# Holding both scatter-adds of an expert to one place in the GpSimd queue of a one-core attention and mixture-of-experts kernel

## The chip, the core and the metric

The kernel runs on one core of one Trainium2 chip. The metric is the device time of one launch in microseconds (us), taken as the median of repeated runs. The profile shown here is one separate profiled execution of the same kernel.

## What is computed

The input `x` is 4 x 2048 x 512 float32, so 8192 tokens of 512 numbers. The output is `x` plus two branches, both of which read the layer-normalised tokens `xn`:

- an attention-like branch with 512 random features: `feats = exp(xn . proj - |xn|^2 correction)`, the same for a 512 x 512 weight matrix, and the product of the two;
- a mixture of 64 experts plus one shared expert. The router gives 64 scores per token; the best 4 of 8 groups of experts are kept, then the best 8 experts. An expert has 256 slots (`CAP`), which are given to its tokens in the order of the tokens; later ones are dropped.

In short form:

```python
g = einsum('ech,ehi->eci', dispatch, gate_w)
u = einsum('ech,ehi->eci', dispatch, up_w)
expert_out = einsum('eci,eih->ech', silu(g) * u, down_w)
output = zeros((t, h)).at[tidx].add(expert_out[flat_e, pos_c] * weight)
output += (silu(tokens @ shared_gate_w) * (tokens @ shared_up_w)) @ shared_down_w
x = x + attention(xn) + output
```

`dispatch` holds the tokens' rows sorted to expert and slot. The line with `.at[tidx].add` is the one that the change is about: each expert's 256 result rows are added to the rows of the output that belong to its tokens.

## The kernel before, in words

**Numbers.** All products are float32. An operand is split into an upper part in float32r (`upper`, L98, a ScalarE copy) and the rest (`rest`, L101, a VectorE subtraction), and `products` (L104) does three TensorE matmuls for each product. So TensorE lines in a profile mostly stand at L109, and the two split helpers at L99 and L102; the tiles' names tell what they belong to.

**Stages.** First the tokens are normalised, routed and counted in 16 blocks of 512 (`look_up`, `dense`); for half of the blocks the shared expert and the attention are finished there, for seven of the others the attention is left for later (`late_attention`), and what they need is kept in DRAM. Then comes the expert stage, a loop over `i` from 0 to 64 (L881), with pieces of the left-over attention between the experts. At the end the rest of the blocks is finished (`ends`): it reads the output rows back, adds the shared expert and the attention, and writes them.

**The expert loop.** Iteration `i` traces, in this order: the loads of weights ahead of time; the hidden layer of expert `i` (`hidden`, TensorE, tile `ps_gu`); one step of `slots` (`seek`), which issues two lookups on GpSimd (`find`, L656, tile `at`) for expert `i + 9`; the gather of the token rows of expert `i + 4` (`gather`, L709, tile `xg`, two indirect DMAs of 128 rows, one of four buffers); the transposes of expert `i + 1` (`turn_slots`, L724, tile `ps_t`); a share of the left-over attention; and `down(i - 1)`: for each half of 128 slots the second layer (tile `ps_e`), its scaling by ScalarE into `ye` (L773, three buffers of both halves), and the sum, an indirect DMA that adds the 128 rows to the output in DRAM (L774).

Every fourth step of `seek` also traces `tokens_of` (L664): five VectorE operations that turn the looked-up counts of four experts into the token numbers `who` (L677). This is in iterations 0, 4, 8 and so on up to 56 (and once ahead of the loop), right ahead of the gather that is the first to need these numbers: in iteration 32, for example, the gather of expert 36.

**Who sets the order.** All engines work through their own queue in the order in which a planner at compile time puts the instructions; the planner follows the traced order, its own estimate of when operands are ready, and the dependences that it is given. `behind(a, b)` (L118) gives it an order without a wait at run time: `a` is put after `b` on their engine. `in_turn` (L122) used it to line up the lookups, gathers and sums on the GpSimd queue, each behind the last. The gathers, lookups and sums are all issued from that queue.

**The sums' own dependences.** `chain` (L569) is called at the end of `down` with the two sums of the expert. It declares that the two have no dependence on each other (they add to different rows), with

```python
tc.declare_no_dep(a.ins, b.ins, reason="different rows")
```

and makes each of them wait at run time until both sums of the expert before have landed, since those can share rows. In the kernel before, this declaration comes after `in_turn` has put the second sum behind the first.

Of the kernel before, what the change touches and what calls it, by code (L numbers as in the profile page):

```python
# [54 lines left out]
def rfs_attention_moe_kernel(  # L55
# [48 lines left out]
    def products(ps, w, v, start, stop):  # L104

        n = len(w)
        for part, (a, b) in enumerate(((0, 0), (0, 1), (1, 0))):
            for c in range(n):
                last["pe"] = nc.tensor.matmul(  # L109
                    ps,  # L110
                    w[c][a],
                    v[c][b],
                    start=(start and part == 0 and c == 0),
                    stop=(stop and part == 2 and c == n - 1),
                )
        return last["pe"]

    def behind(a, b):  # L118

        tc.add_manual_dep(a.ins, b.ins.name, ORDER, reason="what a needs comes late")  # L120

    def in_turn(a):  # L122

        if "pool" in last:
            behind(a, last["pool"])
        last["pool"] = a
        return a

    class Chunks:

# [29 lines left out]
    last = {}  # L160
# [408 lines left out]
    def chain(group):  # L569

        for n, a in enumerate(group):
            for b in group[:n]:
                tc.declare_no_dep(a.ins, b.ins, reason="different rows")
            for b in added[-1] if added else ():
                tc.add_manual_dep(a.ins, b.ins.name, AFTER, reason="rows in common")
        added.append(group)
# [75 lines left out]
    def find(at, e):  # L652

        for h in range(NH):
            in_turn(
                nc.gpsimd.indirect_dma_start(  # L656
                    out=at[:, e % TE, h, :],
                    out_offset=None,
                    in_=upto,
                    in_offset=bass.IndirectOffsetOnAxis(ap=line[:, e, h : h + 1], axis=0),  # L660
                )
            )
# [42 lines left out]
    def gather(e):  # L705
        xgs[e] = rows.tile([P, NH, XW], FP, tag="xw", name="xg")
        for h in range(NH):
            in_turn(
                nc.gpsimd.indirect_dma_start(  # L709
                    out=xgs[e][:, h, :],  # L710
                    out_offset=None,
                    in_=xnw,
                    in_offset=bass.IndirectOffsetOnAxis(ap=who[:, e, h : h + 1], axis=0),
                )
            )
# [44 lines left out]
    def down(e, hp, w):  # L760
        dh, dl = w
        group = []
        ye = yes[e % len(yes)]
        for h in range(NH):
            po = ps_mm.tile([P, H], FP, tag="mm", name="ps_e")
            products(
                po,
                [(hp[:, 0, c, ts(h, P)], hp[:, 1, c, ts(h, P)]) for c in range(IC)],
                [(dh[:, c, :], dl[:, c, :]) for c in range(IC)],
                True,  # L770
                True,
            )
            nc.scalar.activation(ye[:, h, :], po, AF.Copy, scale=wes[e][:, h : h + 1])  # L773
            now = nc.gpsimd.indirect_dma_start(  # L774
                out=out,
                out_offset=bass.IndirectOffsetOnAxis(ap=who[:, e, h : h + 1], axis=0),
                in_=ye[:, h, :],
                in_offset=None,
                compute_op=ALU.add,
            )  # L780
            group.append(in_turn(now))

        chain(group)

    xgs, wes, gps, gates, downs, gws, dws, hps = ({} for _ in range(8))

# [94 lines left out]
    for i in range(E + 1):  # L881


        if i + 2 < E:
            gates[i + 2] = load_gates(i + 2)
        if i + 1 < E:
            downs[i + 1] = load_down(i + 1)
        if i < E:
            hps[i] = hidden(i, gps.pop(i), gws.pop(i))
        next(slots, None)  # L890
        if i + 4 < E:
            gather(i + 4)
        if i + 1 < E:
            gps[i + 1] = turn_slots(i + 1)
            gws[i + 1] = split_gates(gates.pop(i + 1))
        for _ in range(rest_steps * i // E, rest_steps * (i + 1) // E):
            next(rest_of, None)
        if i >= E - 2:
            next(last_of)
        if i == E:  # L900

            next(last_of)
        if i > 0:
            down(i - 1, hps.pop(i - 1), dws.pop(i - 1))
        if i < E:
            dws[i] = split_down(downs.pop(i))
# [40 lines left out]
```

## Time and profile before

| | |
|---|---|
| median of 3 runs | 1384.04 us (1380.48 to 1386.56) |
| the profiled execution | 1387.8 us |
| its span, first to last instruction | 1385.9 us |
| TensorE matmul busy | 1336.9 us (96% of the span) |
| VectorE busy | 933.5 us (67%) |
| ScalarE busy | 673.7 us (49%) |
| GpSimd busy | 580.8 us (42%) |
| mean granted TensorE clock | 0.99 of full speed |
| share of the 16 DMA engines' span taken by packets issued from SyncE / from GpSimd | 51.7% / 26.7% |
| expert stage: first and last sum issued | 487.3 us / 1236.1 us |

A matmul's end is modelled in the profile, so busy TensorE time is not the same as TensorE at its peak; gaps in it, however, are real. Times within the profile are counted from the start of the span. For an indirect DMA, the busy time is that of the issuing GpSimd instruction, and the landing of the data comes later. "Idle before ... <- X" means that the engine did nothing for so long, and that X was the last event before it went on; a wait for several things is put down to the last of them.

### The profile page before, as it was taken

To read this page: it belongs to the slowest core of one execution; us is meant where nothing else is said; L and a number is where in the kernel's file an instruction comes from. 1 tells how busy PE (TensorE), PEld (TensorE's weight loads), DVE (VectorE), ACT (ScalarE), POOL (GpSimd) and SP (SyncE) were. 2 spreads that over 40 slices of the span, in tenths; PEclk is the share of its full clock that TensorE was granted. 3 is DMA by queue.
4 is the path that set the end of the run, shared out by engine and by line. 5 is a ranking of instruction groups with operands and counts; after the bars stand their busy time and mean duration, and the time that the engine had idled before them with its cause. 6 is when DMAs were issued, how large, how long until landed. Compare 5 with 4: busy or idle time off the path is not lost.

```text
span 1385.9 us, 23019 instructions
## 1 busy us (share of the span) xinstructions
PE 1336.9 (96%) x8416; PEld 1200.2 (87%) x8416; DVE 933.5 (67%) x2026; ACT 673.7 (49%) x1153; POOL 580.8 (42%) x683
## 2 busy tenths in 40 slices
PE   7899999999999999999999999899997999999998
PEld 5788888888888899999999998799987999987886
DVE  5886768768766577776777676567765776644455
ACT  5544444443532466565656565465654565631111
POOL 3321121101103567677657767656675664320000
PEclk9999999999999999999999999999998999999999
DMA  7555454654556999999999989899998898857895
GB/s 241 186 205 174 186 196 152 224 186 150 202 198 184 300 253 275 244 292 261 255 269 295 270 235 269 220 278 240 313 241 242 216 316 237 243 110 281 278 324 202
DMA packets 198032, 327.17 MB, mean 236 GB/s; under 512 B 15648, under 2 KB 103456, under 8 KB 197920
## 3 DMA queue, kind: packets, MB, share of 16 engines
q1 hardware_dynamic: 165152, 245.93, 51.7%
q0 software_dynamic: 32768, 79.78, 26.7%
q8 instruction: 66, 1.08, 0.3%
q14 instruction: 46, 0.38, 0.1%
HBM read 220.66 MB, written 104.99 MB: 235 GB/s over the span
## 4 chain that ended last, share of the span: by engine, by line
PE 76%; DVE 9%; DMA 5%; ACT 4%; POOL 2%; issue 2%; SPq 0%; DVEq 0%; POOLq 0%; ACTq 0%
PE ps_gu L109 36%; PE ps_e L109 11%; PE ps_o L109 9%; PE ps_fu L109 5%; PE ps_y L109 5%; PE ps_t L724 4%; PE ps_f L109 3%; PE ps_l L331 2%; DMA xg<-xnw,who 2%; DVE st L261 1%; PE ps_x L303 1%; DMA at<-upto,line 1%; ACT xw L280 1%; DMA xo<-out_dram 1%; DMA xnw<-xw 1%
## 5 line engine op out<-in xcount | busy, mean ns | idle before, releaser
L774 POOL DMA_INDIRECT out_dram<-ye,who x128 | 224.8, 1756 | 206.8 <-DMA out_dram<-ye,who 36.8
L109 PE MATMUL ps_gu<-gT,gu_h 128*128 128x256 f32 x2048 | 295.2, 286 | 1.3 <-DVE gT L102 1.3
L109 PEld LDWEIGHTS ps_gu<-gT,gu_h 128*128 128x128 f32 x2048 | 270.9, 193 | 8.0 <-DVE gT L102 1.9
L656 POOL DMA_INDIRECT at<-upto,line x128 | 145.1, 1133 | 91.6 <-DVE first_of L650 52.9
L109 PE MATMUL ps_gu<-gT,gu_l 128*128 128x256 f32 x1024 | 165.9, 284 | 0.1
L709 POOL DMA_INDIRECT xg<-xnw,who x128 | 142.2, 1111 | 50.5 <-issue 42.1
L102 DVE TENSOR_TENSOR gu_l<-gu,gu_h 128x1024 fp32r<-128x1024 f32 x128 | 155.3, 1215 | 1.5 <-ACT gu_h L99 1.3
L109 PE MATMUL ps_e<-d_h,ehT 128*128 128x512 f32 x512 | 148.4, 391 | 0.0
L109 PEld LDWEIGHTS ps_gu<-gT,gu_l 128*128 128x128 f32 x1024 | 141.7, 193 | 0.3 <-DVE gu_l L102 0.3
L99 ACT CAST gu_h<-gu 128x1024 fp32r<-128x1024 f32 x128 | 131.4, 1058 | 0.0
L230 POOL TENSOR_TENSOR a<-rstd,ve 128x4 f32<-128x4 f32 x48 | 11.1, 232 | 273.4 <-DVE rstd L228 270.7
L99 ACT CAST ehT<-sg 128x512 fp32r<-128x512 f32 x64 | 39.7, 621 | 171.4 <-DVE sg L464 171.4
L469 ACT ACTIVATE f<-f,ab 128x256 f32<-128x256 f32 x128 | 65.1, 509 | 97.2 <-DVE f L456 94.7
L773 ACT ACTIVATE ye<-ps_e,we 128x512 f32<-128x512 f32 x128 | 88.4, 694 | 42.7 <-PE ps_e L109 41.9
L109 PEld LDWEIGHTS ps_e<-d_h,ehT 128*128 128x128 f32 x512 | 93.3, 188 | 17.2
L464 DVE SCALAR_TENSOR_TENSOR sg<-sg,ps_gu 128x512 f32<-128x512 f32 x64 | 44.0, 687 | 76.1 <-PE ps_gu L109 76.1
L463 DVE SCALAR_TENSOR_TENSOR sg<-sg,ps_gu 128x512 f32<-128x512 f32 x64 | 43.9, 685 | 73.9 <-ACT sg L462 73.1
L724 PE MATMUL ps_t<-ident,xg 128*128 128x128 f32 x512 | 73.9, 277 | 16.7 <-DMA xg<-xnw,who 15.5
L102 DVE TENSOR_TENSOR d_l<-d,d_h 128x1024 fp32r<-128x1024 f32 x64 | 78.2, 1221 | 15.5 <-ACT d_h L99 15.5
L109 PE MATMUL ps_o<-fW_h,fT 128*128 128x512 f32 x288 | 81.0, 395 | 3.1 <-ACT fT L99 3.0
L102 DVE TENSOR_TENSOR gT<-ps_t,gT 128x512 fp32r<-128x512 f32 x128 | 83.3, 682 | 0.4 <-ACT gT L99 0.4
L109 PE MATMUL ps_o<-d_h,hT 128*128 128x512 f32 x256 | 79.8, 395 | 0.0
(170 smaller groups left out, 2683.1 us busy)
## 6 DMA issues: line engine op xcount, KB each, us to landing
gu<-in_L_ffn_gate_w_dram SPq DMA_DIRECT2D x64, 512.0 KB
gu<-in_L_ffn_up_w_dram SPq DMA_DIRECT2D x64, 512.0 KB
d<-in_L_ffn_down_w_dram SPq DMA_DIRECT2D x64, 512.0 KB
xnw<-xw SPq DMA_DIRECT2D x32, 577.0 KB
xb<-in_L_attn_x_dram SPq DMA_DIRECT2D x32, 512.0 KB
out_dram<-xb SPq DMA_DIRECT2D x32, 512.0 KB
xu<-turned SPq DMA_DIRECT2D x28, 512.0 KB
turned<-xT_h SPq DMA_DIRECT2D x16, 512.0 KB
```

The source lines that it names most:

```text
L99: return nc.scalar.copy(dst, src)
L102: return on.tensor_tensor(dst, src, hi.bitcast(FP), ALU.subtract)
L109: last["pe"] = nc.tensor.matmul(ps, w[c][a], v[c][b], start=(start and part == 0 and c == 0), stop=(stop and part == 2 and c == n - 1),)
L331: logits = nc.tensor.matmul(pl, rwp[:, kc].rearrange("p t e -> p (t e)"), v[kc], start=(n == 0 and kc == 0), stop=(n == 1 and kc == KC - 1),)
L463: nc.vector.scalar_tensor_tensor(dst, dst, 1.0, g, ALU.add, ALU.mult)
L464: nc.vector.scalar_tensor_tensor(dst, dst, 0.5, u, ALU.mult, ALU.mult)
L469: nc.scalar.activation(f, f, AF.Exp, scale=ab[:, rc : rc + 1])
L656: nc.gpsimd.indirect_dma_start(out=at[:, e % TE, h, :], out_offset=None, in_=upto, in_offset=bass.IndirectOffsetOnAxis(ap=line[:, e, h : h ...
L709: nc.gpsimd.indirect_dma_start(out=xgs[e][:, h, :], out_offset=None, in_=xnw, in_offset=bass.IndirectOffsetOnAxis(ap=who[:, e, h : h + 1], ...
L724: turned_s = nc.tensor.transpose(ps[:, c, ts(h, P)], xg[:, h, ts(c2 * 2 + c, P)], ident)
L773: nc.scalar.activation(ye[:, h, :], po, AF.Copy, scale=wes[e][:, h : h + 1])
L774: now = nc.gpsimd.indirect_dma_start(out=out, out_offset=bass.IndirectOffsetOnAxis(ap=who[:, e, h : h + 1], axis=0), in_=ye[:, h, :], in_o ...
```

## The change

`in_turn` takes a group of instructions instead of one. Each of the group is put behind every one of the group before; within a group no order is given. Lookups and gathers are still groups of one. The two sums of an expert are now one group, handed over after `chain`.

```diff
-    def in_turn(a):
-
-        if "pool" in last:
-            behind(a, last["pool"])
-        last["pool"] = a
-        return a
+    def in_turn(*group):
+
+        for a in group:
+            for b in last.get("pool", ()):
+                behind(a, b)
+        last["pool"] = group
...
                 compute_op=ALU.add,
             )
-            group.append(in_turn(now))
+            group.append(now)
 
         chain(group)
+        in_turn(*group)
```

No instruction is added or removed; the data that each one reads and writes is the same.

## The prediction

> **What bounds the kernel now.** I read the page first (busy times, chain), then the waits, the stages, and the timelines of TensorE and GpSimd around the two places that stood out.
>
> ```profile
> PE 1336.9 (96%) x8416; PEld 1200.2 (87%) x8416; DVE 933.5 (67%) x2026; ACT 673.7 (49%) x1153; POOL 580.8 (42%) x683
> PE 76%; DVE 9%; DMA 5%; ACT 4%; POOL 2%; issue 2%; SPq 0%; DVEq 0%; POOLq 0%; ACTq 0%
> ```
>
> TensorE bounds the kernel: busy 96%, and 76% of the chain that ended last. So GpSimd's order counts only where TensorE waits for it. The waits, in total, number and longest:
>
> ```profile
> PE ps_t L724 <- DMA xg<-xnw,who: 15.5, 5, 7.4
> POOL out_dram L774 <- DMA out_dram<-ye,who: 36.8, 12, 4.6
> ```
>
> The first is TensorE waiting for a gather, nearly all of it in two waits of over 7 us. The stages (TensorE busy first, clock and DMA share last) show where:
>
> ```profile
> 480.00:860.00 380.00, 379.08 (x2679) 355.25 (x2678) 273.58 (x433) 227.56 (x347) 256.09 (x190) 1.00 0.97 268
> 860.00:880.00 20.00, 12.66 (x82) 11.63 (x81) 8.06 (x12) 7.10 (x11) 12.62 (x10) 0.83 0.79 188
> 1050.00:1070.00 20.00, 12.37 (x82) 11.31 (x82) 12.01 (x18) 10.12 (x15) 10.44 (x9) 0.84 0.81 232
> ```
>
> Outside these two windows the expert stage keeps TensorE full. Inside each it stands still and then runs at a lower clock. TensorE at the first, then GpSimd:
>
> ```profile
> 864.78 0.28 PE L109 MATMUL ps_fu<-xu,pT_h 128*128 128x256 f32 x1
> 872.20 0.45 PE L724 MATMUL ps_t<-ident,xg 128*128 128x128 f32 x1 [7.15 <-DMA xg<-xnw,who]
> ```
> ```profile
> 849.16 2.38 POOL L774 DMA_INDIRECT out_dram<-ye,who  x1 [0.30 <-ACT d_h L99]
> 851.85 1.01 POOL L656 DMA_INDIRECT at<-upto,line  x1 [0.30 <-issue]
> 853.17 0.98 POOL L656 DMA_INDIRECT at<-upto,line  x1 [0.30 <-issue]
> 857.94 2.02 POOL L774 DMA_INDIRECT out_dram<-ye,who  x1 [3.79 <-ACT gu_h L99]
> 860.27 0.99 POOL L656 DMA_INDIRECT at<-upto,line  x1 [0.30 <-DVE f L456]
> 861.56 0.95 POOL L656 DMA_INDIRECT at<-upto,line  x1 [0.30 <-issue]
> 862.82 0.94 POOL L709 DMA_INDIRECT xg<-xnw,who  x1 [0.30 <-issue]
> 864.06 0.95 POOL L709 DMA_INDIRECT xg<-xnw,who  x1 [0.30 <-issue]
> 865.31 1.63 POOL L774 DMA_INDIRECT out_dram<-ye,who  x1 [0.30 <-issue]
> 867.25 1.77 POOL L709 DMA_INDIRECT xg<-xnw,who  x1 [0.31 <-issue]
> 869.32 1.20 POOL L709 DMA_INDIRECT xg<-xnw,who  x1 [0.30 <-issue]
> ```
>
> Counting pairs, 862.82/864.06 is the gather of expert 36, for which TensorE waits, and 857.94/865.31 are the two sums of expert 31, traced behind that gather (iteration 32). One sum stands ahead of the gather and even ahead of the next lookups. It waited 3.79 us at the head of the queue; the named ScalarE cast is only the last event, since by the semaphore events the sum at 849.16 landed at 857.14. So the declaration in `chain` undid the order between the two sums: the first had nothing behind it, the second nothing ahead of it. Over the whole stage, 14 of 64 experts have their sums split, experts 3, 7, ... 55: exactly those whose iteration's gather needs fresh token numbers from L677, late in the planner's eyes. At 1050 to 1070 it is the same: split sums of expert 47, gather 52 issued at 1057.7, wait 7.43 us.
>
> [...] nothing passes the sum waiting until 857.94. [...] Here sums of most experts begin 0.8 to 0.9 us after the previous landing. [...] Here 1.62 us against 7.6 us to landing (medians), 7.0 for a gather. [...] The clock record shows 0.5 from 869.0 to 875.8 and from 1063.5 to 1073.8.
>
> **The sums are a second chain, as long as TensorE's.** Sum, sum 1.92 us later, landing 7.6, restart 0.8: 10.3 us at the least. The mean from one expert's first sum to the next's, experts 8 to 59, is 10.9 where the pair is together and 15.8 where it is split, as the landing starts only with the late half. Four experts take 15.8 + 3 x 10.9 = 48.5 us. TensorE's pace is the first scaling's end (486.4) to the last expert's (1234.0), less 19.8 of stalls (below), over 63: 11.55, so 46.2 for four. GpSimd loses 2.3 per four experts. The lag from `ye` ready to sum indeed grows from 6.8 (expert 8) to 21.9 (expert 32), and the gathers behind it lose their lead: last issue of gathers 8, 12, 16 to first transpose is 21.8, 21.7, 17.2 us; of gather 32, 6.2; of gather 36, 1 us before TensorE wanted it.
>
> **The change part by part.** Instructions and bytes: none added, 0 us.
> *Second sum put behind the gather, first sum put ahead of the lookups.* In 50 of 64 experts this is the order already: 0. At expert 31: lookups end at 854.15, gathers at 854.45 and 855.7; `who` was written by 846.1 and the buffer free at 822.6, so no wait. Landing at 855.7 + 7.0 = 862.7, longest seen 9.5 gives 865.2, against 865.06 where TensorE wants it. At expert 47: lookups end 1047.9, gathers 1048.2 and 1049.4, landing 1056.4 (at most 1058.9) against 1059.92. Both stalls go even with the lag unchanged.
> *The lag.* Without splits four experts take 43.6 us at most against 46.2, so lag no longer builds up, and leads should stay near the early 20 us.
> *What is now held.* Behind both sums stand the next lookups and gather: 1.9 us more where a pair was split, while the next gather (867.25) comes at about 864. Behind the gather stand the sums: where there is no lag, the gather waits for `who`, written 2.5 to 3.8 us after `ye` (expert 3: 516.9 to 519.9; expert 11: 609.0 to 612.7), then two gathers of 1.25 and a gap: sums at most 6.6 us after `ye`. The surplus of 0.65 to 1.25 us per expert (11.55 less 10.9 or 10.3) works that off, largely, before the next group. It is hidden by the gathers' lead of 20 us; if that is gone, each such gather costs a stall like those above. `ye` has three buffers, 35 us, and does not bind.
> *What is late next.* Nothing seen: TensorE was full from 500 to 860 at a DMA share of 0.97, so the loads keep up with this pace. After 1236 the tail is TensorE's and just starts earlier.
>
> The sum: idle 7.15 + 7.43 = 14.58. Half clock after them: 3.6 us busy (872.2 to 875.8) and 6.4 (1067.4 to 1073.8), half of each lost, 1.8 + 3.2 = 5.0. Together 19.6 to 19.8; cross-check: from 865.06 to 880.9, 8 transposes and 48 matmuls (0.87 + 5.76 us elsewhere in the chain) take 15.8, a loss of 9.2; from 1059.92, 17.2, a loss of 10.6. Two small gaps may go too: 0.53 at 1017 (gather 48) and 0.92 at 842.6, where VectorE waited for late lookups; I leave them as the low end. The profiled execution goes from 1387.8 to 1368.0, its span from 1385.9 to 1366.1. The runs' median lies 3.8 below that execution: 1384.04 - 19.8 = **1364.2**.
>
> **Rivals.**
> *One stall stays.* The gathers of experts 32, 36, 48 and 52 had the least lead, also because TensorE's queue asks for these rows early; if some lag stays, a landing of up to 9.5 us leaves no margin at 36. Half the gain: about 1374. Against it: the lag should be gone by then.
> *No gain.* The planner's splits were its answer to late token numbers; held, GpSimd waits for `who` in 14 iterations, and landings of 8.4 us instead of 7.6 bring the sums' pace to TensorE's. Lag then builds up as before: 1384. Or the order was not lost in the way I read it. Against: splits at every fourth expert and nowhere else.
> *Slower.* The wait for `who` takes the place of the split, and the new constraint moves the planner's order of the token operations on VectorE back; the gather then leads by less than its 7.0 us landing. A stall with its half clock costs 9.9; two cancel the gain, from the third it is slower. With four of the 14 groups: 1364.2 + 39.6 = 1404; with three, 1394. For it: the plan of all engines is made anew. Against: a lead of 20 has 13 us to spare.
>
> **How the numbers follow.** Both stalls gone 0.60 (own range 1360 to 1368); one stays 0.13, of which 0.12 beyond 0.5%; no gain 0.11; slower 0.16, of which 0.01 is within 0.5%. 0.5%, or 6.9 us, is about what a measurement of this kernel can tell from no change. Faster 0.72, same 0.13, slower 0.15. The low end, 1359, takes both small gaps (1362.7) and some more; the high end, 1387, takes in one stall and no gain, leaving out about 0.15 above and 0.05 below.
>
> **What would show it.** No split pair among the 64; no wait of TensorE for `xg` over 1 us; no half clock between 500 and 1240; sums at most some 7 us behind `ye`, not growing; gathers leading by 15 us or more; GpSimd idle ahead of L709 for `who`, of 1 to 4 us, at up to 14 gathers. I am wrong if splits remain, if lag still grows, or if TensorE waits newly for `gT`, `ye` or weights.

## The result and the profile after

The kernel after takes 1365.48 us (median of 6 runs, 1363.51 to 1369.83) against 1383.92 us for the kernel before (6 runs, 1380.48 to 1386.56). The ratio is 0.9877, 95% interval 0.9855 to 0.9899: 18.4 us, or 1.2%, faster. The forecast was 1364.2 with a range of 1359 to 1387. The profiled execution took 1365.37 us, with a span of 1363.3 us.

Compared instruction by instruction in the two traces, TensorE's 8416 matmuls, VectorE's 2026 instructions and ScalarE's 1153 start in the same order, and so do the 564 transfers in SyncE's queue. GpSimd's 683 alone have another order: none of the 64 experts has its sums split. So the two traces differ by that order and by the waits that follow from it.

Busy times and the chain that ended last, from the page of the kernel after:

```profile
PE 1329.8 (98%) x8416; PEld 1194.8 (88%) x8416; DVE 933.1 (68%) x2026; ACT 673.9 (49%) x1153; POOL 592.3 (43%) x683
PE 81%; DVE 9%; DMA 4%; ACT 3%; POOL 2%; issue 2%; SPq 1%; POOLq 0%; DVEq 0%; ACTq 0%
```

TensorE's share of the chain rose from 76% to 81%. The gathers' transfers, 2% of the chain before, are no longer among the lines that the page lists for it. The two windows in which TensorE had stood still (TensorE busy first, granted clock, DMA share and GB/s last):

```profile
860.00:880.00 20.00, 20.00 (x147) 18.78 (x146) 14.58 (x23) 13.08 (x20) 15.60 (x12) 1.00 0.83 201
1050.00:1070.00 20.00, 20.00 (x141) 18.70 (x140) 15.14 (x21) 11.74 (x19) 15.58 (x12) 1.00 0.91 239
```

Both are full, at full clock (1.00, where it had been 0.83 and 0.84). Of TensorE's waits, longest in total first, these head the list; the wait for `xg`, 15.5 us before, is not on it at all:

```profile
PE ps_l L331 <- ACT cu L429: 8.8, 14, 1.4
PE ps_x L303 <- ACT xw L280: 6.6, 5, 4.5
```

The iteration of expert 36's gather, first on GpSimd and then on TensorE:

```profile
844.93 0.95 POOL L709 DMA_INDIRECT xg<-xnw,who  x1 [4.84 <-issue]
846.68 1.00 POOL L709 DMA_INDIRECT xg<-xnw,who  x1 [0.80 <-issue]
847.99 1.81 POOL L774 DMA_INDIRECT out_dram<-ye,who  x1 [0.30 <-issue]
850.11 1.59 POOL L774 DMA_INDIRECT out_dram<-ye,who  x1 [0.30 <-issue]
852.00 1.02 POOL L656 DMA_INDIRECT at<-upto,line  x1 [0.30 <-issue]
```
```profile
862.99 0.28 PE L109 MATMUL ps_fu<-xu,pT_h 128*128 128x256 f32 x1
863.11 0.62 PE L724 MATMUL ps_t<-ident,xg 128*128 128x128 f32 x4
```

The gather is issued at 844.93 and 846.68 instead of 862.82 and 864.06; the rows are there when TensorE wants them at 863.11, and no time lies between the attention's matmul and the transposes. The 4.84 us ahead of the gather are a new wait of GpSimd: VectorE finished `who` (L677) at 844.2. The page calls it "issue" since it names no releaser. Right behind the gather stand both sums of expert 31. Their lag is 7.6 us, where it had been 16.7. Here and below, lag is the time from the end of the scaling of an expert's first half into `ye` to the start of the first of its sums, and lead is the time from the start of a gather's second DMA to the first transpose of its rows.

The expert stage, from the end of the first expert's first scaling into `ye` to that of the last expert's, went from 486.4 to 1234.0 (747.6 us) to 485.6 to 1211.6 (726.0 us): 21.6 us, nearly all of the span's 22.6. Most of the rest is 0.8 us that lie ahead of the first sum, where the kernels do not differ.

### The profile page after: what moved, and what is told of

The parts are those of the page before. It is cut to its first block, busy times and chain, and to the rows that moved or that the text cites. A ratio compares the mean times of both kernels' runs of the same rounds, so it can differ in the third digit from the quotient of the medians.

```text
span 1363.3 us, 23061 instructions
## 1 busy us (share of the span) xinstructions
PE 1329.8 (98%) x8416; PEld 1194.8 (88%) x8416; DVE 933.1 (68%) x2026; ACT 673.9 (49%) x1153; POOL 592.3 (43%) x683
## 3 DMA queue, kind: packets, MB, share of 16 engines
q0 software_dynamic: 32768, 79.78, 26.2%
## 4 chain that ended last, share of the span: by engine, by line
PE 81%; DVE 9%; DMA 4%; ACT 3%; POOL 2%; issue 2%; SPq 1%; POOLq 0%; DVEq 0%; ACTq 0%
PE ps_gu L109 38%; PE ps_e L109 13%; PE ps_o L109 9%; PE ps_y L109 6%; PE ps_fu L109 6%; PE ps_t L724 4%; PE ps_f L109 3%; PE ps_l L331 2%; DVE st L261 1%; PE ps_x L303 1%; ACT xw L280 1%; DMA xo<-out_dram 1%; DMA xnw<-xw 1%; ACT f L469 1%; DMA xT_l<-turned 1%
## 5 line engine op out<-in xcount | busy, mean ns | idle before, releaser
L774 POOL DMA_INDIRECT out_dram<-ye,who x128 | 216.2, 1689 | 121.0 <-DMA out_dram<-ye,who 25.6
L709 POOL DMA_INDIRECT xg<-xnw,who x128 | 151.1, 1180 | 103.5 <-issue 96.8
L656 POOL DMA_INDIRECT at<-upto,line x128 | 155.6, 1216 | 91.6 <-DVE first_of L650 52.9
L102 DVE TENSOR_TENSOR d_l<-d,d_h 128x1024 fp32r<-128x1024 f32 x64 | 78.2, 1221 | 15.5 <-ACT d_h L99 15.5
L109 PE MATMUL ps_e<-d_l,ehT 128*128 128x512 f32 x256 | 79.2, 390 | 0.0
```

The source lines that it names most:

```text
L102: return on.tensor_tensor(dst, src, hi.bitcast(FP), ALU.subtract)
L109: last["pe"] = nc.tensor.matmul(ps, w[c][a], v[c][b], start=(start and part == 0 and c == 0), stop=(stop and part == 2 and c == n - 1),)
L656: nc.gpsimd.indirect_dma_start(out=at[:, e % TE, h, :], out_offset=None, in_=upto, in_offset=bass.IndirectOffsetOnAxis(ap=line[:, e, h : h ...
L709: nc.gpsimd.indirect_dma_start(out=xgs[e][:, h, :], out_offset=None, in_=xnw, in_offset=bass.IndirectOffsetOnAxis(ap=who[:, e, h : h + 1], ...
L774: now = nc.gpsimd.indirect_dma_start(out=out, out_offset=bass.IndirectOffsetOnAxis(ap=who[:, e, h : h + 1], axis=0), in_=ye[:, h, :], in_o ...
```

## The experiments

Two readings of the stalls were to be told apart. The **lag theory**, on which the forecast rests: a split makes an expert's sums land late, the next expert's sums wait for that landing, and the delay adds up over many experts until what stands behind the sums in GpSimd's queue comes too late for TensorE. The rival, **place alone**: a sum in front of the gather holds it back there and then, whatever came before. Where nothing else is said, TensorE's, VectorE's and ScalarE's queues keep the order of the kernel after.

**Two splits of fourteen.** The kernel after, with the old dependences for experts 31 and 47:

```diff
         chain(group)
-        in_turn(*group)
+        if e in (31, 47):
+            for b in last["pool"]:
+                behind(group[0], b)
+            last["pool"] = group[1:]
+        else:
+            in_turn(*group)
```

> The kernel after, but the sums of experts 31 and 47 alone are left as before (the first only behind the gather, only the second ahead of the next lookups). These are the two splits right ahead of the two stalls of the kernel before. All other engines keep their order. Lag theory (a stall needs the delay of the sums that the splits before it have piled up): no wait of TensorE for xg over 1 us, no half clock in the expert stage, 1363 to 1368 us. Rival, place alone (a split just ahead of a gather that is wanted early makes the stall, whatever came before): both stalls return, about 1385 us.

Measured: 1364.34 us (ratio to the kernel before 0.9847, 95% interval 0.9812 to 0.9881; so in this order below). GpSimd around the first split:

```profile
845.13 1.62 POOL L774 DMA_INDIRECT out_dram<-ye,who  x1 [4.76 <-DMA out_dram<-ye,who]
...
849.74 0.95 POOL L709 DMA_INDIRECT xg<-xnw,who  x1 [0.30 <-PE ps_fu L109]
850.99 0.95 POOL L709 DMA_INDIRECT xg<-xnw,who  x1 [0.30 <-issue]
852.24 1.62 POOL L774 DMA_INDIRECT out_dram<-ye,who  x1 [0.30 <-issue]
```

The order is that of the kernel before, with an even longer wait at the head of the queue (4.76 us against 3.79). But the lag is 4.4 us where it was 16.7, and the gather leads its first transpose by 12.4 us. Without the split it leads by 16.4, so one split takes 4 us of the lead, which is not enough for a stall. TensorE has no wait for `xg`, and no half clock like that of the stalls shows: the mean granted clock of the execution is 0.997, against 0.990 in the kernel before and 0.998 in the kernel after. Place alone falls.

**Twelve splits of fourteen.** The same edit with `if e not in (31, 47)`.

> The other way round: the kernel before with its 14 split pairs, except that the sums of experts 31 and 47 are held together. Lag theory: two of 14 splits fewer save GpSimd 2 x 4.9 us, about the price of one stall; the lag still builds up, gathers 36 and 52 are in time, but a wait for xg returns at another gather of a fourth expert (40 to 60): 1370 to 1380 us. Rival, place alone: no stall is left, 1363 to 1368 us.

Measured: 1372.19 us (0.9907, 0.9873 to 0.994). The two gathers that had been late are in time, the lag climbs to 24.6 us, and TensorE loses time elsewhere. From the waits of all engines (total, number, longest):

```profile
DVE at L668 <- DMA at<-upto,line: 3.6, 3, 1.6
...
PE ps_gu L109 <- DVE gT L102: 3.1, 4, 1.2
...
PE ps_t L724 <- DMA xg<-xnw,who: 1.2, 1, 1.2
```

The wait for `xg` is back at the gather of expert 48 (lead 2.4 us), as the theory had it. But most of the waiting is a kind that I had not expected: VectorE stands at L668, the first operation on the looked-up counts, for lookups that have not landed, and the rest of `gT`, for which TensorE waits, is behind it in VectorE's queue. The lookups sit behind the sums just as the gathers do (in the kernel after, above, the lookup at 852.00 comes right behind the sum at 850.11).

**Late landings without a split.** The kernel after; at experts 3, 7, ... 55 the second sum waits for the first one's landing (`AFTER` stands for a wait at run time). The order on every engine is unchanged.

```diff
             for b in group[:n]:
-                tc.declare_no_dep(a.ins, b.ins, reason="different rows")
+                tc.add_manual_dep(a.ins, b.ins.name, AFTER, reason="one by one") if len(added) % 4 == 3 and len(added) < 56 else tc.declare_no_dep(a.ins, b.ins, reason="different rows")
```

> The kernel after, with the queue order of every engine unchanged and no split; at experts 3, 7, ... 55 the second sum also waits until the first has landed. That makes the landing of these 14 experts late by about 6.5 us, as a split did with 4.9, without any change of order. Lag theory: four experts take GpSimd 16.8 + 3 x 10.9 = 49.5 us against TensorE's 46.2, the lag grows by 3.3 per four, after some 4 to 6 groups the lead of the gathers is used up and TensorE waits for xg in several places: 1378 to 1400 us, most likely 1388. Rival (the order of the queue itself cost the time): no stall, 1363 to 1368 us.

Measured: 1398.64 us (1.011, 1.0069 to 1.0151). Delay alone, with the queues in the new order, costs all of the gain and more. The four executions spread from 1387.1 to 1404.2 us, and the trace is of the shortest. In it the lag climbs to 26.2 us. The time lies in the range of the lag theory, near its top; the place is not the expected one: TensorE waits 1.3 us for `xg` in all, and 9.3 us for `gT`. From the waits:

```profile
PE ps_gu L109 <- DVE gT L102: 9.3, 9, 1.8
...
DVE at L668 <- DMA at<-upto,line: 8.9, 4, 2.8
...
DVE at L668 <- DMA xg<-xnw,who: 3.9, 2, 3.3
```

The third line names a gather, as the last event before VectorE went on; the operation at L668 reads lookups alone. The two runs below test that.

**The lookups as the way.** First the same kernel with `LEAD = 13`, so that lookups come four iterations earlier.

> The run with 14 late landings (the second sum of experts 3, 7, ... 55 after the first has landed) with the lookups four iterations earlier. There most of TensorE's lost time was not at xg but at gT: VectorE's queue stood at L668 for late lookups, with the rest of gT behind it. If the late lookups were the way by which the lag reached TensorE, the waits at L668 go, the lag grows past 25 us, and the gathers become the next to be late: TensorE waits for xg in two or three places of 7 us; 1375 to 1395 us. Rival (the waits at L668 were late for another reason): they stay, and the time stays near 1399.

Measured: 1403.21 us (1.0128, 1.0064 to 1.0192). The waits at L668 did not go: they are 26.8 us in all, against 12.8 in the run above, with one of 7.1 us at 468.1, ahead of the first sum. The expectation was badly made: the step that issues the lookups also traces the token operations, so these moved along, and the distance between the two was the same. The run tells nothing of the lookups. In the second one only the lookups move:

```diff
-LEAD = 9
+LEAD = 13
...
-        for e in range(E + TE):
+        for e in range(E + 2 * TE):
...
-            if k == 1 and n:
+            if k == 1 and n in (1, 2):
                 tokens_of(n - 1, ats.pop(n - 1), last["dve"])
+            if k == 1 and n > 3:
+                tokens_of(n - 2, ats.pop(n - 2), last["dve"])
```

> As the run with 14 late landings (LEAD 9), but the lookups of an expert are issued four iterations earlier while the token operations on VectorE stay in the iteration where they were (in the run before this one they had moved together, so that their distance had not changed). If lookups that land late are what held VectorE at L668, these waits go (from 12.8 us in the first of these runs to under 2 us) and the waits for gT with them (from 9.3 to under 3 us); the sums stay as slow, so the lag grows past 25 us and the gathers are the next to be late: TensorE waits for xg, two or three times by some 7 us; 1375 to 1395 us. Rival (VectorE waits at L668 for something else): the waits stay and the time stays near 1399.

Measured: 1400.26 us (1.0124, 1.0059 to 1.019). From the waits (L726 is the transpose, two lines further down in this kernel):

```profile
PE ps_t L726 <- DMA xg<-xnw,who: 19.3, 13, 3.8
...
DVE at L668 <- DMA at<-upto,line: 7.0, 1, 7.0
```

One wait at L668 is left, of 7.0 us, near the start of the stage, before any sum; the waits for `gT` are gone. In their place the gathers are late, 13 times. The lag reaches 28.5 us. So late lookups were what had held VectorE. The time did not fall, against my 1375 to 1395. In these two runs the planner also gave other engines a new order, which costs some time ahead of the stage (TensorE idle for 5.34 and 5.25 us before the first sum), so their times are not to be compared with the others' to a few us. The expert stage by itself is not shorter in the traces either: 753.3 us here, 746.6 in the run with 14 late landings (there the shortest execution). That fits the reading, without proving it, that with late landings the sums are the slower chain, and that which of their followers fails first decides only where TensorE waits.

**Splits without the wait.** The kernel before, with its 14 splits; the sums of odd experts go to a side buffer of 256 rows, and each expert's sums wait for those of two experts back. The output leaves out the odd experts.

```diff
-                out=out,
-                out_offset=bass.IndirectOffsetOnAxis(ap=who[:, e, h : h + 1], axis=0),
+                out=side if e % 2 else out,
+                out_offset=bass.IndirectOffsetOnAxis(ap=slot_i[:, h : h + 1] if e % 2 else who[:, e, h : h + 1], axis=0),
...
-            for b in added[-1] if added else ():
+            for b in added[-2] if len(added) > 1 else ():
```

> The kernel before with its splits, but the sums of odd experts go to 256 rows of a side buffer (so the output leaves out the odd experts), and an expert's sums wait for those two experts back instead of one. The splits stay; the landing of the expert before no longer holds the queue. Lag theory: the sums follow ye within 10 us to the end, no wait of TensorE for xg over 1 us: 1362 to 1368 us. Rival (the order of the queue itself cost the time): the stalls stay, about 1384 us.

Measured: 1365.34 us (0.9859, 0.9824 to 0.9895). All 14 pairs are split, as expert 31's here:

```profile
841.56 2.32 POOL L774 DMA_INDIRECT side<-ye,slot_i  x1 [6.07 <-ACT ye L773]
...
850.21 1.63 POOL L774 DMA_INDIRECT side<-ye,slot_i  x1 [0.30 <-issue]
854.70 1.62 POOL L774 DMA_INDIRECT out_dram<-ye,who  x1 [0.30 <-issue]
```

The next expert's sum goes out 4.5 us after the late half, and it waits for nothing. In the kernel before it came 9.8 us after the late half (865.31), and it waited for the landing:

```profile
875.14 1.62 POOL L774 DMA_INDIRECT out_dram<-ye,who  x1 [4.62 <-DMA out_dram<-ye,who]
```

The lag never passes 5.2 us. With the wait for the landing out of the way, the split costs nothing. (Next to the kernel before, a few instructions of TensorE, ScalarE and VectorE stand in another order here.)

**Why pairs were split.** The kernel before, without the change, with `LEAD = 10`: lookups and token operations one iteration earlier.

> The kernel before, not the change, with every lookup issued one iteration earlier (LEAD 10 for 9), so that the token numbers are there one iteration before the gather that needs them first. If the splits come from token numbers that are late in the planner's eyes, no pair is split although nothing holds it, the sums follow ye within 10 us, and the time is that of the kernel after: 1362 to 1369 us. Rival (the splits have another cause, such as the lookups' place or the buffers): splits and stalls stay, about 1384 us.

Measured: 1369.3 us (0.9895, 0.9839 to 0.9952). No pair is split though nothing holds one, and the lag is 2.5 us at most: the splits do come from token numbers that the planner sees arriving after the sums. (The lookups moved as well, but they stand in every iteration, and the splits stood in every fourth.) GpSimd's order is the same with and without the change then (the kernel with both was built, not run). Next to the kernel before, the planner gives the other engines a new order, too. The time is 0.3 us above the expected range. This kernel pays once, ahead of the first sum, where the token operations come before their lookups have landed; from VectorE's waits:

```profile
DVE at L668 <- DMA at<-upto,line: 7.0, 1, 7.0
```

TensorE stands still for 4.0 us at 463.5, and the mean granted clock of the execution is 0.995, against 0.998 in the kernel after.

**The sums as the only bound.** The kernel after with all pairs one by one (`AFTER` for every pair; the order on TensorE and GpSimd is unchanged).

> The kernel after with the second sum of every expert waiting until the first has landed; TensorE's queue and GpSimd's are unchanged. The sums' chain alone then gives the pace: 2 x (7.6 + 0.8) = 16.8 us per expert against TensorE's 11.55. Lag theory: the last sum at about 486 + 63 x 16.8 = 1545 us, and the end some 150 us later: 1690 us (1640 to 1740). If landings were no second chain, the time would stay near 1365.

Measured, in one run: 1627.08 us; the last sum went out at 1475.6. From the waits, and then the stage as a whole (columns as above):

```profile
DVE at L668 <- DMA at<-upto,line: 132.4, 13, 14.1
...
PE ps_gu L109 <- DVE gT L102: 92.2, 27, 10.9
...
PE ps_t L724 <- DMA xg<-xnw,who: 68.7, 40, 9.0
```
```profile
480.00:1480.00 1000.00, 820.35 (x5228) 756.03 (x5226) 528.14 (x828) 441.14 (x671) 469.98 (x354) 0.90 0.75 193
```

Both ways of being late are there at full size, and a third: with a lag of up to 39.9 us the three buffers of `ye` no longer suffice, and ScalarE waits 103.9 us, in 35 waits, for sums to land. The sums give the pace: 15.8 us from expert to expert. I had expected 16.8, and a total of 1640 to 1740, so the forecast was too high. Two of its terms were off, in opposite directions. The landing took 7.1 us for a first sum and 5.9 for a second in the mean (6.0 in the median of all), not 7.6, as far as the trace tells the landings (81 of 128). From the second landing to the next sum it took 1.6 us, not 0.8: lookups and gathers stand between the two in the queue. The DMA engines are busy 0.75 of this stage, against 0.93 of the stage in the kernel before.

## Why the prediction was right, point by point

- **The order that was lost.** Right. All splits are gone, and two sums that keep no order among themselves are enough. Lining up the two one by one after the declaration, not before it, gives every engine its old order again (this kernel was built, not run): the declaration removes the order whichever comes first.
- **Two stalls and their half clock, 19.8 us.** Right: the kernel after has neither (its granted clock is 1.00 from 486 to 1212 us, TensorE busy for 725.95 of these 726.00), and the expert stage is 21.6 us shorter. The two small gaps that I left for the low end (0.53 and 0.92 us) went too, 21.3 in all. The forecast of the span was 1366.1, it is 1363.3; that of the runs 1364.2, it is 1365.5. That the last two lie so close is partly luck. The profiled executions differ by 22.4 us and the medians by 18.4: the profiled execution of the kernel before was longer than all six of its timed runs, and the distance of 3.8 us to the median, which the forecast carried over, is not there in the kernel after (0.1).
- **The second chain.** Right, and the point that carries the rest: on one chip, two splits at the very places of the stalls gave 1364.3 us, twelve elsewhere 7.9 us more, and 14 late landings in the new order 34.3 us more. The mean from first sum to first sum, experts 8 to 59, is 11.4 us now, close to TensorE's pace (11.52); it was 12.1.
- **What is now held.** Nearly right. I gave the sums 6.6 us behind `ye` at most; those behind a held gather reach 7.8, because GpSimd starts 0.75 us after `who` is written and the two gathers take up to 3.1 us, not 2.5. A few others come later still; the latest is expert 28's with 8.7, after a landing of 9.6 us. GpSimd is idle ahead of the gathers of experts 8, 12, ... 60 for 1.2 to 7.6 us, not 1 to 4. It doesn't matter: from expert 8 on no gather leads by less than 16.4 us.
- **What was incomplete.** I followed the lag to TensorE by the gathers alone. The lookups are a second way, over VectorE's queue, and `ye` is a third once the lag is long enough. In the kernel before the second one showed only as the gap of 0.92 us at 842.6, which I had named without drawing that conclusion.
- **The rivals.** One stall staying, and no gain, would have needed the lag to persist; it doesn't. For the slower one the planner would have had to reorder other engines; their order didn't change at all.

## What to carry to other kernels

A run-time wait between successive transfers, here "land before the next may add to the same rows", can make a chain of its own. Here its period was 15.8 us per expert where each pair went one by one, with landings of 7.1 and 5.9 us (means) in it. Compare such a period with the period of the engine that bounds the kernel, and do it over the whole stage, since a deficit of 2 us per four experts needed half the stage to show. When a late transfer appears in front of the bounding engine, look for how its lead shrank over time rather than only at what stands ahead of it in its queue. An order that is given and then a dependence that is declared away should be checked against the queue that comes out.

## What the runs showed of the hardware that was not expected

- The granted clock was lower with much shorter waits than the 7 us of the kernel before. In the run with 14 late landings TensorE's longest wait, apart from those ahead of `ps_x` that the kernel after has too (5.1 us at most, 5.6 there), was 1.8 us (for `gT`, 9 waits with 9.3 us in all). The mean granted clock of that execution was 0.991, against 0.998 in the kernel after, and about as low as in the kernel before with its two stalls (0.990).
- Where TensorE stood still more, it was lower over a whole stage: in the run with all pairs one by one, TensorE was busy for 820 of the 1000 us from 480 to 1480, and the granted clock was 0.90. In the kernel after it was busy for 755.4 of the 756 us from 480 to 1236, at 1.00. How much idle time it takes to lower the clock was not shown.
- The landing of the same 128-row sums, each issued by a GpSimd instruction of 1.62 us (median, in all three traces named here), took 6.0 us in the median where the DMA engines were busy 0.75 of the stage, and 7.6 and 8.0 where it was 0.93 and 0.94 (the kernels before and after; for the latter the trace tells 81 of 128). That the two sums of a pair fly one at a time in the first case need not be the reason. Within the kernel before, among sums that overlapped another, the 22 during whose flight the DMA engines were busy for less than 0.85 landed in 5.1 us (median), the 70 with 0.95 or more in 8.2 us.
